# The order of the two readers of a score tile in the masked layers of a cross-attention stack

## Chip, cores and metric

The kernel runs on one core of a Trainium2 chip. The metric is device time in microseconds (us). Five engines work side by side, each through its own instructions in order: TensorE (PE in the profile; its weight loads are PEld), VectorE (DVE), ScalarE (ACT), GpSimd (POOL) and SyncE (SP, which issues DMAs). Semaphores hold an instruction back until those of other engines that it depends on are done.

## What is computed

Four cross-attention layers follow one another on an activation `x` of 2048 rows by 256, all of them attending to the same context of 1601 rows by 512. Layers 0, 2 and 3 are the masked ones; layer 1 is a grouped-query layer with an RMS norm. Cut to what matters here, a masked layer is:

```python
q = (x @ Wq).reshape(...)          # 16 heads of 64
k = (ctx @ Wk).reshape(...); v = (ctx @ Wv).reshape(...)
logits = einsum('bhqd,bhkd->bhqk', q, k) * 64 ** -0.5
col_bias[:, token_indices_A] = -20 * (1 - mask_A)[:, None]
col_bias[:, token_indices_B] = -20 * (1 - mask_B)[:, None]
probs = softmax(logits + col_bias, axis=-1)
x = (probs @ v).reshape(...) @ Wo + bo + x
```

All values are float32.

## The kernel before

**Tiling.** The activation stays in SBUF, transposed (`xT`). A masked layer is cut into 8 blocks, each a pair of heads `n`, and a block into 4 units, each 512 query rows; so there are 24 masked blocks and 96 masked units, and 32 units of the grouped layer. Scores are computed transposed: 128 keys on the partitions, and two heads by 512 queries in the free dimension. The keys of a layer, 1601 and 12 extra columns for the biased tokens, make `NT` = 13 key tiles (the last is shorter). `exc` holds a very negative number for the keys that a layer must leave out, so the score tile is never used without adding a column of `exc`.

**One key tile of a unit** passes through these steps:
- `front` (L393 to L411, matmuls L401; for the last key tile also the bias rows, L408): PE writes the score tile `s` in PSUM.
- `front_act` (L414): ACT copies the score tile to a slot `p` of an SBUF ring (L422). For key tile 0 it is instead an activation that adds `exc` (L418).
- `front_dve` (L424): DVE takes the running maximum, `top = max(s + exc, top)` (L430). For key tile 0 there is none; key tile 1 takes `p` of key tile 0 in place of `top`.
- `subtract`: 16 steps later DVE adds the negative maximum, spread over PSUM tile `mb`, to `p` in place (L461; L459 for key tile 0).
- `exp_act` and `exp_pool`: 18 steps later ACT takes the exponential in place (L467), and POOL adds it to `sums` (L473 for the first two tiles, L475 after).
- `attend`: 20 steps later PE multiplies it with the values into `po` (L483).

The score tile thus has two readers on two engines, L422 and L430. They are never run at the same time on one tile: whichever is written second in the program waits for the first, and the next `front` that uses the buffer waits for both.

**Other work of a unit.** PE transposes `top` (L439), DVE reduces it to `ntop` (L444), PE spreads it (L450) into `mb`. At the end of a unit ACT takes `po` out (`take`, L490); PE sums the exponentials over the keys (`row_pe`, L496); ACT evacuates them (`row_act`, L503), and they go through DRAM (`dens`) to a reciprocal on DVE (L512) and back into `rx`; POOL multiplies `o` by it (L523). PE then multiplies by `Wo` (`out_pe`, `halves`, L301) in two parts, and DVE adds each to `xT` (L566). The queries of a later unit are a matmul of `xq` (L301) that ACT scales into `qT` (L390). The keys and values of the next block are made meanwhile as "fill" pieces (L301), evacuated by ACT into `kT` (L351) and `v` (L371). In the last block of each layer the row piece is replaced by another form (`den_pe`, `den_act`, `scale_pe`).

**Buffers.** PSUM holds two score tiles (`ps_s`), one `mb`, one `po` and a single buffer `pm`, which all the smaller products share: a `pm` matmul waits until the one before it has been evacuated. The ring has 22 slots; a copy waits until POOL and PE have used what the slot held 22 tiles ago. There is one `sums`, so L473 of a unit waits for L496 of the unit before.

**Order.** Masked operations are pinned to program order (`pin`), and that order is written out by hand in the loop over `pair` (from L1060). A pair is two steps, so two key tiles; 13 pairs make two units. A small planner puts at most one piece in the middle of a pair (`mid`, `m` in the loop) and one at its end (`end`, `e`), by fixed offsets within the unit and, for fill, by how much is due. A piece has a PE part and may have a DVE part and an ACT part. The order within a pair, before the change, is: both fronts (PE); both `front_act` (ACT); sometimes one subtraction; the first `front_dve`; the middle piece's PE and DVE parts; the second `front_dve`; the middle piece's ACT part (`m.act`); the attends and `take`; the end piece's PE and DVE parts; the exponentials and sums; the end piece's ACT part; the subtractions. What stands on one engine runs in this order.

Of the kernel before, what the change touches and what calls it, by code (L numbers as in the profile page):

```python
# [38 lines left out]
def tile_cross_attention_stack(ctx: ExitStack, tc: tile.TileContext, t: dict, out: bass.AP):  # L39
# [874 lines left out]
    def at_step(s, offset):  # L914

        w, c = divmod(s - offset, NT)
        return (units[w], c) if 0 <= w < NU else None
# [127 lines left out]
    def plan_queries(w):  # L1045
        def pe():
            un = unit(w)
            un.qpe, un.qthen = un.layer.queries(un)
            un.qpe()

        if made[w // NB].layer.grouped:
            early.setdefault((NT * w - (2 if w % 32 == 0 else 12)) // 2, []).append(lambda: fetch(w))
            return
        early.setdefault(max(NT * w - 18, 0) // 2, []).append(lambda: fetch(w))
        place(end, NT * w - 6, Piece(1024, pe, act=lambda: units[w].qthen()))
# [4 lines left out]
    for pair in range((END + 1) // 2):  # L1060
        steps = [2 * pair, 2 * pair + 1]
        for s in steps:
            w, c = divmod(s, NT)
            if c == 0 and w < NU:
                i, b = divmod(w, NB)
                if b == 0:
                    made[i].layer.load_out(made[i])
                if b == 0 and i + 1 < len(blocks):
                    l, n = blocks[i + 1]
                    while i and fill:  # L1070
                        _, pe, then = fill.popleft()
                        pe()
                        then()
                    made[i + 1] = layers[l].load(n)
                    new = layers[l].fill(made[i + 1])
                    fill.extend(new)
                    total = sum(f[0] for f in fill)

                    hold = 9 if i and layers[blocks[i - 1][0]].grouped and n == 1 else 1
                    pace = total / (NB * NT / 2 - 3 - hold)  # L1080
                    due = -pace * hold
                    spent = 0.0
                plan(w)
                for v in ([1, 2] if w == 0 else [w + 2]):
                    if v < NU:
                        plan_queries(v)
        fronts = [at_step(s, 0) if s < NT * NU else None for s in steps]
        subs = [at_step(s, SUB) for s in steps]
        exps = [at_step(s, EXP) for s in steps]
        vals = [at_step(s, VAL) for s in steps]  # L1090
        fronts = [f for f in fronts if f]
        subs = [f for f in subs if f]
        exps = [f for f in exps if f]
        vals = [f for f in vals if f]

        due += pace
        if fill and spent + fill[0][0] <= due + 400:
            slot = mid if pair not in mid else end if pair not in end else None
            if slot is not None:
                cost, pe, then = fill.popleft()  # L1100
                spent += cost
                slot[pair] = Piece(cost, pe, act=then)
        m, e = mid.pop(pair, None), end.pop(pair, None)

        lead = len(vals) == 2 and vals[0][1] == NT - 1
        if lead:
            un, c = vals.pop(0)
            un.layer.attend(un, c)
            un.layer.take(un)
        for thunk in early.pop(pair, []):  # L1110
            thunk()
        grouped_back = [f for f in subs if f[0].layer.grouped]
        all_grouped = bool(fronts) and all(f[0].layer.grouped for f in fronts) and all(
            f[0].layer.grouped for f in subs) and bool(subs)
        for f in fronts + grouped_back:
            f[0].alone = all_grouped
        for i in range(2):
            for f in fronts[i : i + 1]:
                f[0].wide = False
                f[0].layer.front(*f)  # L1120
            if i == 0:
                for f in grouped_back[:1]:
                    f[0].wide = True
                    f[0].layer.again(*f)
        for f in fronts:
            f[0].layer.front_act(*f)
        for f in subs:
            if not f[0].layer.grouped and f[1] == NT - 1 and f is subs[0]:
                f[0].layer.subtract(*f)
                subs = subs[1:]  # L1130
                break
        for f in fronts[:1]:
            f[0].layer.front_dve(*f)
        if m:
            m.pe()
            if m.dve:
                m.dve()
        for f in fronts[1:]:
            f[0].layer.front_dve(*f)
        if m and m.act:  # L1140
            m.act()
        for un, c in vals:
            un.layer.attend(un, c)
            if c == NT - 1:
                un.layer.take(un)
        for f in grouped_back[1:]:
            f[0].wide = True
            f[0].layer.again(*f)
        if e:
            e.pe()  # L1150
            if e.dve:
                e.dve()
        for f in grouped_back:
            f[0].layer.exp_act(*f)
        for f in exps:
            if not f[0].layer.grouped:
                f[0].layer.exp_act(*f)
                f[0].layer.exp_pool(*f)
        if e and e.act:
            e.act()  # L1160
        for f in subs:
            if not f[0].layer.grouped:
                f[0].layer.subtract(*f)
# [34 lines left out]
```

## Time and profile before

| | |
|---|---|
| median of 3 runs | 4883.03 us (4873.75 to 4885.01) |
| the profiled execution | 4873.81 us |
| its span, first to last instruction | 4872.0 us |
| mean granted TensorE clock | 0.975 of full |
| copies L422 | 1152 of 1014 ns |
| running maxima L430 | 1056 of 1280 ns, and 96 of 1283 ns |
| subtractions L461 | 1152 of 1273 ns |
| exponentials L467 | 1248 of 1059 ns |
| sums on POOL L475 | 1056 of 2371 ns |
| ACT's evacuation of the sums `rx` L503 | 84, 0.6 us each |

The profile shows one execution. Its page gives each engine's busy time and the chain of work that ended last, followed back from the end; its groups put instructions of one line, engine and operation together. The trace behind it answers further views: who waited for whom, a timeline of stretches of time, and busy time by windows with the granted TensorE clock. A bracket in the timeline is the idle time of the engine before the instruction and what ended it.

The masked layers run from about 120 to 1320 us and from about 2320 us to the end; the grouped layer lies between, with both kinds of unit in flight at its edges.

### The profile page before, as it was taken

How to read it: one execution, taken by the hardware profiler on the slowest of the kernel's cores; microseconds unless marked ns; L12 is line 12 of the kernel's file. 1: busy time of each engine (PE TensorE's matmuls, PEld its weight loads, DVE VectorE, ACT ScalarE, POOL GpSimd, SP SyncE). 2: the span in 40 equal slices, each digit the busy share in tenths (PEclk: the TensorE clock that was granted, in tenths of full speed). 3: DMA queues.
4: the chain of work that ended last, by engine and by line, in shares of the span. 5: the costliest groups of instructions: out<-in, count | busy, mean ns of one | idle time of the engine just before them, and what ended most of it. 6: DMA issues, size and time to landing. Idle time of an engine off the chain costs nothing.

```text
span 4872.0 us, 68510 instructions
## 1 busy us (share of the span) xinstructions
PE 4510.9 (93%) x26779; PEld 1883.5 (39%) x26779; DVE 3779.4 (78%) x3687; ACT 3192.2 (66%) x3709; POOL 3012.8 (62%) x1565
## 2 busy tenths in 40 slices
PE   6999999999878989898999999999999999999997
PEld 3433443334333333334433443344433433344332
DVE  3788888888866666654788888888888888888896
ACT  2677676776645555555677666766666776767775
POOL 0677777777751222110677777777777777777787
PEclk8999999999989999999999999999999999999998
DMA  2000010100011000000000010001000001011000
GB/s 82 17 25 26 24 27 25 31 22 27 22 31 32 12 18 19 10 21 20 21 25 23 27 27 25 25 25 27 23 24 20 27 25 31 23 27 27 22 18 18
DMA packets 136793, 121.70 MB, mean 25 GB/s; under 512 B 64033, under 2 KB 103457, under 8 KB 136470
## 3 DMA queue, kind: packets, MB, share of 16 engines
q1 hardware_dynamic: 125238, 103.50, 7.8%
q0 software_dynamic: 9120, 11.72, 1.2%
q8 instruction: 212, 3.47, 0.3%
q10 hardware_dynamic: 2112, 2.10, 0.1%
q14 instruction: 111, 0.91, 0.1%
HBM read 103.16 MB, written 14.09 MB: 24 GB/s over the span
## 4 chain that ended last, share of the span: by engine, by line
PE 76%; ACT 10%; DVE 6%; POOL 4%; issue 3%; DMA 1%; POOLq 0%; SPq 0%; ACTq 0%; DVEq 0%
PE pm L301 21%; PE s L401 20%; PE po L483 17%; PE po L830 4%; ACT p L822 3%; ACT p L422 3%; DVE top L430 3%; POOL sums L473 2%; PE pm L439 2%; PE mb L450 2%; POOL sums L475 2%; PE s L760 1%; ACT p L467 1%; PE s L809 1%; DVE p L461 1%
## 5 line engine op out<-in xcount | busy, mean ns | idle before, releaser
L475 POOL TENSOR_TENSOR sums<-sums,p 128x1024 f32<-128x1024 f32 (+1 forms) x1056 | 2503.6, 2371 | 372.4 <-ACT p L467 319.7
L430 DVE SCALAR_TENSOR_TENSOR top<-s,exc,top 128x1024 f32<-128x1024 f32 (+1 forms) x1056 | 1351.7, 1280 | 408.3 <-ACT p L422 373.0
L422 ACT COPY p<-s 128x1024 f32<-128x1024 f32 (+1 forms) x1152 | 1129.4, 1014 | 664.5 <-PE s L401 461.8
L461 DVE SCALAR_TENSOR_TENSOR p<-p,exc,mb 128x1024 f32<-128x1024 f32 (+1 forms) x1152 | 1418.1, 1273 | 0.0
L401 PE MATMUL s<-qT,kT 64*128 64x512 f32 (+1 forms) x4992 | 1280.3, 622 | 94.8 <-DVE top L430 93.9
L467 ACT ACTIVATE p<-p 128x1024 f32<-128x1024 f32 (+1 forms) x1248 | 1255.2, 1059 | 23.2 <-DVE p L461 22.0
L483 PE MATMUL po<-p,v 128*64 128x512 f32 (+1 forms) x4992 | 1207.7, 600 | 3.5 <-ACT p L467 2.7
L401 PEld LDWEIGHTS s<-qT,kT 64*128 64x128 f32 (+1 forms) x4992 | 418.1, 184 | 774.5 <-issue 317.9
L473 POOL TENSOR_TENSOR sums<-p 128x1024 f32<-128x1024 f32 x96 | 226.8, 2363 | 732.2 <-PE pm L496 544.5
L483 PEld LDWEIGHTS po<-p,v 128*64 128x64 f32 (+1 forms) x4992 | 341.0, 138 | 540.8 <-issue 441.6
L775 DVE TENSOR_REDUCE gtop<-s 128x2 f32<-128x1024 f32 x261 | 316.8, 1221 | 123.7 <-PE s L760 122.5
L301 PE MATMUL pm<-wv,ctxT 128*64 128x128 f32 (+1 forms) x4992 | 361.5, 283 | 48.1 <-ACT rx L503 45.6
L742 POOL DMA_DIRECT2D qT<-gqueries x256 | 123.9, 492 | 454.9 <-PE s L814 296.3
L301 PEld LDWEIGHTS pm<-wv,ctxT 128*64 128x64 f32 (+1 forms) x4992 | 287.8, 139 | 203.4 <-issue 100.9
L822 ACT ACTIVATE p<-s 128x1024 f32<-128x1024 f32 (+1 forms) x267 | 270.1, 1023 | 138.8 <-PE s L814 134.8
L301 PE MATMUL pm<-ctxT,wk 128*64 128x256 f32 (+1 forms) x2688 | 314.2, 377 | 8.3 <-ACT rx L503 4.8
L301 PEld LDWEIGHTS pm<-ctxT,wk 128*64 128x64 f32 x2688 | 172.6, 140 | 199.3 <-issue 75.9
L830 PE MATMUL po<-p,v 128*32 128x512 f32 (+1 forms) x1664 | 245.3, 621 | 1.9 <-ACT rx L842 1.6
L301 PE MATMUL pm<-o,wo 128*64 128x512 f32 x768 | 205.2, 611 | 10.2 <-POOL o L523 6.1
L775 DVE TENSOR_REDUCE gtop<-mb 128x2 f32<-128x1024 f32 x123 | 150.3, 1222 | 75.1 <-PE mb L760 74.5
L444 DVE TENSOR_REDUCE ntop<-pm 128x4 f32<-128x512 f32 x192 | 131.8, 687 | 97.5 <-PE pm L439 97.1
L822 ACT ACTIVATE p<-mb 128x1024 f32<-128x1024 f32 (+1 forms) x149 | 152.5, 1024 | 77.9 <-PE mb L814 75.7
(165 smaller groups left out, 3226.4 us busy)
## 6 DMA issues: line engine op xcount, KB each, us to landing
xq<-snap SPq DMA_DIRECT2D x84, 512.0 KB
rx<-dens SPq DMA_DIRECT2D x168, 128.0 KB
qT<-gqueries POOLq DMA_DIRECT2D x256, 32.0 KB, 2.0
wk<-in_L_xattn_Wk_dram SPq DMA_DIRECT2D x24, 256.0 KB
wv<-in_L_xattn_Wv_dram SPq DMA_DIRECT2D x24, 256.0 KB
snap<-xT SPq DMA_DIRECT2D x12, 512.0 KB
gqueries<-xq SPq DMA_DIRECT2D x16, 256.0 KB
kT<-gkeys POOLq DMA_DIRECT2D x16, 200.2 KB, 3.9
```

What stands on the lines that cost most here:

```text
L301: pin(nc.tensor.matmul(to[a:e], weights_ap[:, a:e], moving, **kw))
L401: pin(nc.tensor.matmul(s[:m, h, :], u.kT[r, c * P : c * P + m], w.q[r, :], start=True, stop=(c < NT - 1),))
L422: pin(nc.scalar.copy(w.p[c][:m], w.s[c][:m]))
L430: pin(nc.vector.scalar_tensor_tensor(w.top[:m], w.s[c][:m], self.exc[:m, c : c + 1], before[:m], ALU.add, ALU.max,))
L461: pin(nc.vector.scalar_tensor_tensor(p, p, self.exc[:m, c : c + 1], w.mb[:m], ALU.add, ALU.add))
L467: pin(nc.scalar.activation(w.p[c][:m], w.p[c][:m], AF.Exp))
L473: pin(nc.gpsimd.tensor_tensor(w.sums, w.p[0], w.p[1], ALU.add))
L475: pin(nc.gpsimd.tensor_tensor(w.sums[:m], w.sums[:m], w.p[c][:m], ALU.add))
L483: pin(nc.tensor.matmul(w.po[r, :], w.u.v[:m, c, r], w.p[c][:m, h, :], start=(c == 0), stop=(c == NT - 1),))
L775: pin(nc.vector.tensor_reduce(w.top[:, :, q, k : k + 1], w.s[i], AX.X, ALU.max))
L822: pin(nc.scalar.activation(w.p[c][:m], w.s[c][:m], AF.Exp))
L830: pin(nc.tensor.matmul(w.po[ts(j, 32), :], self.v[:m, c, w.u.g, :], w.p[c][:m, h, :], start=(c < 2), stop=(c >= NT - 2),))
```

## The change

For each of the two score tiles of a pair, the running maximum (`front_dve`) now stands first and the copy (`front_act`) directly behind it, in place of both copies ahead of both maxima. Nothing else is written differently; for the grouped layer `front_act` does nothing.

```diff
@@ -1122,8 +1122,6 @@
                 for f in grouped_back[:1]:
                     f[0].wide = True
                     f[0].layer.again(*f)
-        for f in fronts:
-            f[0].layer.front_act(*f)
         for f in subs:
             if not f[0].layer.grouped and f[1] == NT - 1 and f is subs[0]:
                 f[0].layer.subtract(*f)
@@ -1131,12 +1129,14 @@
                 break
         for f in fronts[:1]:
             f[0].layer.front_dve(*f)
+            f[0].layer.front_act(*f)
         if m:
             m.pe()
             if m.dve:
                 m.dve()
         for f in fronts[1:]:
             f[0].layer.front_dve(*f)
+            f[0].layer.front_act(*f)
         if m and m.act:
             m.act()
         for un, c in vals:
```

The copy of a tile now depends on the maximum of that tile, where the maximum depended on the copy. A maximum of key tile 1 still needs the activation of key tile 0.

## The prediction

> **What bounds the kernel now.** I read the page first: busy times, then the chain that ended last.
>
> ```profile
> PE 4510.9 (93%) x26779; PEld 1883.5 (39%) x26779; DVE 3779.4 (78%) x3687; ACT 3192.2 (66%) x3709; POOL 3012.8 (62%) x1565
> PE 76%; ACT 10%; DVE 6%; POOL 4%; issue 3%; DMA 1%; POOLq 0%; SPq 0%; ACTq 0%; DVEq 0%
> ```
>
> TensorE (PE) is busy 93% and holds 76% of the chain. The masked layers alone, in the table by windows (us, then busy time of PE, PEld, DVE, ACT, POOL), are tighter still:
>
> ```profile
> 2500.00:2900.00 400.00, 383.63 (x2268) 160.90 (x2266) 331.33 (x300) 279.06 (x327) 295.81 (x131) 0.98 0.10 26
> ```
>
> PE 96%, DVE 83%, ACT 70%. So a change can give back at most the 4% that PE idles, but can cost as much as it makes PE wait. Who makes PE wait stands in the list of waits (total us, times, longest):
>
> ```profile
> DVE top L430 <- ACT p L422: 444.1, 330, 22.5
> ...
> PE s L401 <- DVE top L430: 93.9, 80, 7.6
> ...
> PE pm L301 <- ACT rx L503: 60.8, 63, 2.4
> ```
>
> The first is what the change removes: the maximum (L430) waits for the copy (L422) of its own score tile. It is idle time of DVE, not of PE. The second is PE waiting for a score buffer (there are two), which the maximum frees as last reader; the third is PE waiting for the single `pm` buffer.
>
> **The change.** In the instruction streams of both builds the counts agree, DVE's order and PE's order are the same, and the waits swap: each maximum waits for PE instead of ACT, each copy waits for DVE instead of PE. ACT's order is the same too, except that one square root of the grouped layer's norm comes a copy (1.0 us) earlier. On POOL three loads of that layer pass one sum, far from its bound (67 of 400 us busy in 1900 to 2300). On SP, 39 loads of `xq` go ahead of a read of `dens`; such a load waits until the queries have read the old `xq`, and the reciprocal that needs the read comes 7 us later on DVE (2817.03 to 2824.60), which covers it; uncovered, each would cost at most the 1 us by which the read is issued later, 39 in all. I count all three at nothing. So the whole price is who is late. Rows: maximum 1.28 us, copy 1.01, exponential 1.06, subtraction 1.27; back to back on one engine they start 1.19, 0.91, 0.96 and 1.19 apart, two dependent maxima 1.39. A handover from ACT to DVE takes 0.03 us (chain, below); from DVE to ACT none is shown; between 0.03 and the 0.24 that a weight load takes after DVE I take 0.04.
>
> *With both engines free* nothing changes: copy, maximum, maximum ends as late as maximum, maximum, copy (3.7 us). *With ACT late* the new order frees the buffer up to 1.3 us sooner. *With DVE late* the copy, until now done in DVE's shadow, is put behind the maximum: the buffer comes free 1.0 us later, and everything queued behind the copies on ACT (evacuating `pm`, the exponentials) comes later by up to 2 to 4 us. DVE is the fuller engine, so I followed one turn of the schedule, 13 pairs of steps (two units, about 80 us), pair by pair, with the durations above. Nine pairs hide it: for example at 2817.36 copies end at 2822.8 instead of 2820.5, the next front needs that buffer at 2823.8, and the exponentials end at 2825.1, before their products at 2826.8. Four do not.
>
> ```profile
> 2804.16 1.99 PE L401 MATMUL s<-qT,kT 64*128 64x512 f32 x8
> ...
> 2807.09 2.66 DVE L430 SCALAR_TENSOR_TENSOR top<-s,exc,top 128x1024 f32<-128x1024 f32 x2
> ...
> 2808.07 0.37 ACT L351 COPY kT<-pm 128x256 f32<-128x256 f32 x1 [0.75 <-PE pm L301]
> ...
> 2809.57 1.03 PE L301 MATMUL pm<-o,wo 128*64 128x512 f32 x4
> ...
> 2814.07 2.67 DVE L430 SCALAR_TENSOR_TENSOR top<-s,exc,top 128x1024 f32<-128x1024 f32 x2 [0.35 <-ACT p L422]
> ...
> 2814.83 0.61 ACT L503 COPY rx<-pm 128x512 f32<-128x512 f32 x1
> ...
> 2815.49 1.94 PE L301 MATMUL pm<-xq,wq 128*64 128x512 f32 x8 [0.25 <-ACT rx L503]
> ```
>
> (1) The front at 2804.16. DVE's maxima of the pair before, with the `xT` addition between them, end at 2802.8 and 2804.6; the second copy then ends at 2805.7, where PE wanted that buffer at 2805.1: **+0.6**. (2) The exponentials follow until 2807.6; this pair's maxima end at 2808.2 and 2809.5 (DVE first does two subtractions), the copies at 2809.2 and 2810.6, the `kT` copy behind them at 2810.9 instead of 2808.4. PE's output matmul needs that `pm` at 2809.6 + 0.6: **+0.7**. (3) That matmul now ends at 2811.9, so the addition, two subtractions and two maxima on DVE run to 2817.6; the second copy to 2818.7, the `rx` copy to 2819.2 instead of 2815.4. PE's queries wait for `pm`: 2819.2 against 2815.5 + 1.3 already lost: **+2.4**, a standstill of 2.7 us. Sum 3.7.
>
> ```profile
> 2837.84 1.27 DVE L430 SCALAR_TENSOR_TENSOR top<-s,exc,top 128x1024 f32<-128x1024 f32 x1
> ...
> 2839.64 1.27 DVE L430 SCALAR_TENSOR_TENSOR top<-s,exc,top 128x1024 f32<-128x1024 f32 x1
> ...
> 2841.06 1.13 PE L401 MATMUL s<-qT,kT 64*128 64x512 f32 x4 [0.71 <-DVE top L430]
> ```
>
> (4) Here DVE is behind (three subtractions, an addition), and PE already waits 0.71 us. The copies were done at 2836.7; now they start at 2839.2 and 2840.95, so the two fronts begin at 2840.2 and 2842.0: **+0.94**. The exponentials end at 2843.9, the next copies at 2845.7, `kT` at 2845.9; where the piece is the short one (77 columns) the output matmul waits **0.5** more. In the next pair DVE's subtractions wait for that matmul; maxima end at 2852.65, the second copy at 2853.7, the `v` copy at 2854.0, and the queries, ready at 2852.4, wait **1.65**. Sum 2.6 or 3.1, mean 2.9.
>
> A turn loses 3.7 + 2.9 = 6.6 us. There are 96 masked units, 48 turns; I take 46, since the last block of a layer has another row piece and the last of all no fill: **46 x 6.6 = 304 us**.
>
> What it gains: the chain once per two turns,
>
> ```profile
> 2938.93 2.35 POOL sums L473
> ...
> 2941.31 1.02 ACT p L422
> ...
> 2942.36 1.29 DVE top L430
> ...
> 2943.70 1.13 PE s L401 x4
> ```
>
> a copy waits for POOL to free a ring slot, the maximum for the copy, PE for the maximum. The maximum would now be done, and PE resumes at 2942.4: 1.3 us sooner, a standstill of 0.85 instead of 2.17. What is late next is POOL's product `o` (L523), which the output matmul needs 16 us on: in blocks where PE ran at full clock after this stall that matmul already waits 0.6 us for it (599.92), so nothing is kept there; where the clock fell, about 1.0 us is. 11 x 1.0 = **-11 us**. The other such chain, which ends in the `rx` copy (the 2.40 us stalls), has no maximum in it and stays.
>
> The clock after a stall, by windows (the figure before the last two is the granted clock):
>
> ```profile
> 2941.50:2944.90 3.40, 1.23 (x8) 0.45 (x8) 2.54 (x3) 3.40 (x5) 3.20 (x2) 1.00 0.00 1
> 2944.90:2948.30 3.40, 3.40 (x18) 1.95 (x18) 3.30 (x3) 1.63 (x2) 3.32 (x2) 0.50 0.04 1
> ```
>
> Of 44 stalls of 2.17 to 2.41 us in the masked layers, 23 are followed by 3.4 us at half clock, 1.7 us each; of the shorter ones (up to 0.79), none. So the 46 new stalls of 2.7 us, a little longer, bring about 46 x 0.55 x 1.7 = **+43 us** (bounds: none, 78 if each does), and the 11 shortened ones that had it (of 22) give back 11 x 1.7 = **-19 us**.
>
> The Trainium skill ("TensorE: Matmul & The Clock Gate", HAM oscillation) warns of idle gaps over about 3.4 us; the rows above fall to half after 2.17. By the page's figure alone both clock terms would be nothing and the sum 5167. The skill also speaks for the wait itself ("PSUM — Partial Sum Buffer", PSUM bank collisions raise a hardware error): ScalarE and VectorE may not read one bank at once; so one reader must wait either way, as both builds do.
>
> **Sum.** The profiled execution took 4873.8 us (span 4872.0), the lowest of the three timed runs being 4873.75 and the median 4883.03. 4873.8 + 304 - 11 + 43 - 19 = 5191; I say **5190**.
>
> **Rivals.**
> A, *faster*: ACT is the late reader, not DVE. Its place is the PE waits behind the maximum, 93.9 us, and the half clock after them, 19: at most -113, so 4761; if only the ring chain gains, 22 x 1.3 + 19 = 48, 4826. It decides if at step (3) the maxima can start over 1 us before the old 2814.07. For it: 444 us of DVE waiting. Against: DVE's additions and subtractions stand between, and most of those waits are 0.35 to 0.6 us in front of an engine with 17% to spare. Chance 0.07.
> B, *no change* (4860 to 4888): the shifts end in PE's slack, as in nine pairs of 13. It needs (1) to (4) each to be over 0.6 to 2.4 us too long. 0.06.
> C, *front waits only*: (1) and (4)'s 0.94 stay, but `pm` comes free in time at (2), (3) and (4): 46 x 1.54 = 71, so 4945; with half of the other 233 some 5060. 0.14.
> D, *more*: each copy's 1.05 us lands on PE in each pair, 624 x 1.05 = 655, so 5530, or delayed exponentials also hold up POOL's sums and `o`: some 5330. 0.07.
> The forecast, 5080 to 5290: 0.66.
>
> **Range.** 5030 to 5290: the forecast with its clock bounds and the upper half of C, short of D. Faster by over 0.3% (about what can be told from no change here) 0.08, within 0.06, slower 0.86.
>
> **What would show it.** Right: DVE's wait for the copy gone from the list, in its place ACT's copy waiting for the maximum with over 400 us; PE waiting for `rx` (L503), `kT`/`v` copies and the score copy with 250 to 350 us in all; standstills of about 2.7 us before the queries, twice a block, with half clock after many; the 2.17 us stalls at 0.9. Wrong: if the queries start without a wait, (3) failed; if fronts wait no longer than 0.71, (4) failed; if the exponentials reach the products late, a fifth place was missed.

## The result and the profile after

The changed kernel takes 5239.74 us (median of 4 runs, 5233.25 to 5241.64) against 4880.42 before: a ratio of 1.0735, with a 95% interval of 1.0716 to 1.0754. It is slower by some 360 us. The profiled execution has a span of 5238.6 us, 366.6 more than that of before.

The page after, busy times and the chain that ended last:

```profile
PE 4592.7 (88%) x26779; PEld 1870.8 (36%) x26779; DVE 3781.8 (72%) x3687; ACT 3198.3 (61%) x3709; POOL 3011.2 (57%) x1565
...
PE 41%; DVE 16%; ACT 9%; issue 4%; POOL 3%; DMA 0%; ACTq 0%; POOLq 0%; DVEq 0%; SPq 0%
```

DVE, ACT and POOL are busy for the same time as before to 6 us: no instruction got dearer. PE is busy 82 us longer with the same 26779 matmuls, and its share of the chain falls from 76% to 41%: the chain now leaves PE often, above all for DVE (16% from 6%).

The list of waits after (total us, times, longest):

```profile
ACT p L422 <- DVE top L430: 1210.9, 920, 6.1
...
DVE top L430 <- PE s L401: 428.1, 226, 8.7
...
PE pm L301 <- ACT rx L503: 164.0, 63, 2.8
...
PE s L401 <- ACT p L422: 116.4, 149, 4.7
```

and, further down the same list, three more waits of PE:

```profile
PE pm L301 <- ACT kT L351: 60.9, 65, 1.7
...
PE pm L301 <- POOL o L523: 42.3, 25, 3.1
...
PE pm L301 <- ACT v L371: 41.4, 45, 1.7
```

The maximum's wait for the copy (444 us) is gone, as the change says. DVE gained nothing: it now waits 428 us for PE. The wait came back on ACT, nearly three times as long, and what stands behind ACT's copies came back as waits of PE: `rx` 164 us from 61, and `kT` and `v` 102 from 5. PE waits for the score buffer 116 us instead of 94.

The place where the forecast put most of the loss, in the timeline after (start, us, engine, line; the last PE row is the queries):

```profile
2984.65 2.67 DVE L430 SCALAR_TENSOR_TENSOR top<-s,exc,top 128x1024 f32<-128x1024 f32 x2
...
2988.31 0.38 ACT L351 COPY kT<-pm 128x256 f32<-128x256 f32 x1
...
2988.74 1.08 PE L301 MATMUL pm<-o,wo 128*64 128x512 f32 x4 [1.02 <-ACT kT L351]
...
2992.85 2.67 DVE L430 SCALAR_TENSOR_TENSOR top<-s,exc,top 128x1024 f32<-128x1024 f32 x2
...
2995.61 1.01 ACT L422 COPY p<-s 128x1024 f32<-128x1024 f32 x1 [0.38 <-DVE top L430]
2996.52 0.59 ACT L503 COPY rx<-pm 128x512 f32<-128x512 f32 x1
...
2997.16 3.27 PE L301 MATMUL pm<-xq,wq 128*64 128x512 f32 x8 [2.70 <-ACT rx L503]
```

The second copy starts when the second maximum ends (2995.5); `rx` starts when ACT is done with the copy; the queries start when `rx` is out. PE stood still 2.70 us, where it was 0.25, and the queries then took 3.27 us instead of 1.94: the clock had fallen. All matmuls of the queries together, from the groups before and then after (busy time and mean duration, then PE's idle time before them and what ended it):

```profile
L301 PE MATMUL pm<-xq,wq 128*64 128x512 f32 x672 | 160.6, 599 | 12.5 <-ACT rx L503 10.4 <-DVE parts L650 2.0
```

```profile
L301 PE MATMUL pm<-xq,wq 128*64 128x512 f32 x672 | 201.4, 729 | 176.7 <-ACT rx L503 113.3
```

Since both kernels run the same matmuls in the same order, the two traces can be laid side by side matmul by matmul, and each growth of the lag put to the place where it arises:

| lag that arises at | us | forecast |
|---|---|---|
| the queries, waiting for `rx`, `kT`, `v` | +170.7 | 46 x (2.4 + 1.65) = 186 |
| the fronts, waiting for the score copy | +61.4 | 46 x (0.6 + 0.94) = 71 |
| the output matmul, waiting for `kT`, `v` | +44.2 | 46 x (0.7 + 0.25) = 44 |
| matmuls without a wait (half clock, above all) | +39.9 | +43 - 19 = 24 |
| the 2.17 us stalls, shortened | -31.8 | with the next row: -11 |
| the output matmul, waiting for POOL's `o` | +37.0 | |
| the edge of grouped and masked layers | +20.2 | none |
| the rest of the grouped layer, and others | +25 | none |

### The profile page after: what moved, and what is told of

Its sections match the earlier page's. It is cut to its first block, busy times and chain, and to the rows that moved or that the text cites. A ratio compares the mean times of both kernels' runs of the same rounds, so it can differ in the third digit from the quotient of the medians.

```text
span 5238.6 us, 68422 instructions
## 1 busy us (share of the span) xinstructions
PE 4592.7 (88%) x26779; PEld 1870.8 (36%) x26779; DVE 3781.8 (72%) x3687; ACT 3198.3 (61%) x3709; POOL 3011.2 (57%) x1565
## 4 chain that ended last, share of the span: by engine, by line
PE 41%; DVE 16%; ACT 9%; issue 4%; POOL 3%; DMA 0%; ACTq 0%; POOLq 0%; DVEq 0%; SPq 0%
PE pm L301 11%; PE s L401 9%; PE po L483 7%; DVE top L430 7%; DVE p L461 6%; PE po L830 4%; ACT p L422 3%; ACT p L822 3%; POOL sums L473 1%; PE s L760 1%; ACT p L467 1%; PE pm L439 1%; POOL sums L475 1%; PE s L809 1%; PE mb L809 1%
## 5 line engine op out<-in xcount | busy, mean ns | idle before, releaser
L422 ACT COPY p<-s 128x1024 f32<-128x1024 f32 (+1 forms) x1152 | 1159.5, 1013 | 1341.9 <-DVE top L430 1210.9
L401 PE MATMUL s<-qT,kT 64*128 64x512 f32 (+1 forms) x4992 | 1298.4, 628 | 118.2 <-ACT p L422 116.4
L822 ACT ACTIVATE p<-s 128x1024 f32<-128x1024 f32 (+1 forms) x267 | 270.1, 1023 | 142.1 <-PE s L814 138.1
L301 PE MATMUL pm<-xq,wq 128*64 128x512 f32 x672 | 201.4, 729 | 176.7 <-ACT rx L503 113.3
L301 PE MATMUL pm<-ctxT,wk 128*64 128x256 f32 (+1 forms) x2688 | 303.6, 368 | 8.4 <-ACT rx L503 4.8
L566 DVE TENSOR_TENSOR xT<-pm,xT 128x512 f32<-128x512 f32 x168 | 115.3, 686 | 216.3 <-PE pm L301 216.2
```

Source lines behind the costliest of these rows:

```text
L301: pin(nc.tensor.matmul(to[a:e], weights_ap[:, a:e], moving, **kw))
L401: pin(nc.tensor.matmul(s[:m, h, :], u.kT[r, c * P : c * P + m], w.q[r, :], start=True, stop=(c < NT - 1),))
L422: pin(nc.scalar.copy(w.p[c][:m], w.s[c][:m]))
L822: pin(nc.scalar.activation(w.p[c][:m], w.s[c][:m], AF.Exp))
```

## The experiments

**e1: the piece's ACT part ahead of the copies.** The maxima stay first; ACT evacuates `pm` before it copies the scores.

```diff
         for f in fronts[:1]:
             f[0].layer.front_dve(*f)
-            f[0].layer.front_act(*f)
+            if f[1] == 0:
+                f[0].layer.front_act(*f)
         if m:
             m.pe()
             if m.dve:
                 m.dve()
+            if m.act:
+                m.act()
+        for f in fronts[:1]:
+            if f[1]:
+                f[0].layer.front_act(*f)
         for f in fronts[1:]:
             f[0].layer.front_dve(*f)
             f[0].layer.front_act(*f)
-        if m and m.act:
-            m.act()
```

> The changed kernel, but ACT runs the middle piece's part (the copies that free pm: rx, kT, v) ahead of the two score copies instead of behind them; maxima still go first. Theory (DVE is the late reader, and most of the loss is pm held up by evacuations queued behind the late copies): the waits for rx, kT and v fall to almost nothing, the 2.7 us standstills and their half clock go, the 2.40 us stall behind the ring goes too; the score-buffer waits of about 1.0 and 0.6 us a turn stay, and qT, now later behind the exponentials, costs up to 0.9. Some 4900 to 5000 us. Rival (the score buffer itself, held 1 us longer by the copy, is the loss): unchanged within 30 us of 5240, since the copies come later still.

Measured 4994.27 us, ratio to before 1.024 (1.0219 to 1.0261), within what the theory gave and 245 us below the changed kernel. Its list of waits:

```profile
ACT p L422 <- DVE top L430: 553.7, 449, 5.2
...
PE s L401 <- ACT p L422: 83.8, 117, 4.7
PE pm L301 <- POOL o L523: 82.6, 82, 3.0
...
PE pm L301 <- ACT qT L390: 42.2, 45, 1.0
...
PE po L483 <- ACT p L467: 36.4, 48, 1.9
```

No wait of PE for `rx` or `kT` stands among them. The rival, the score buffer alone, is out: the copies come later still, and two thirds of the loss are gone. The 245 us are not a clean share of `pm`, though. Laid beside the kernel before, matmul by matmul, e1 has also lost 75 us of waits for `rx` that the kernel before has itself (e4 below takes them out alone), and its own order brings new waits. What the change itself had added at `pm` is the 215 us of the table above (170.7 and 44.2). What is left of the loss (117 us by the traces) lies elsewhere than expected: the exponentials, later still, hold up POOL's sums and with them `o` (82.6 us), and the products with the values (36.4); and evacuating the queries into `qT`, now behind the exponentials, holds up `pm` (lag of 58 us).

**e2 and e3: half of the change.** In e2 the maximum goes first for the first tile of a pair only, in e3 for the second only.

```diff
 # e2
         for f in fronts[1:]:
-            f[0].layer.front_dve(*f)
             f[0].layer.front_act(*f)
+            f[0].layer.front_dve(*f)
...
 # e3
         for f in fronts[:1]:
-            f[0].layer.front_dve(*f)
             f[0].layer.front_act(*f)
+            f[0].layer.front_dve(*f)
```

> One part of the change alone: the maximum goes first for the first tile of each pair, for the second tile the copy stays first. Theory (two engines that hand over to each other in both directions): the second copy stands behind the first copy, which stands behind the first maximum, and the second maximum waits for the second copy, so DVE, which is late already, loses about 1.5 us a pair in addition: by my working 4.3 us in the first half of a turn where the whole change lost 3.7, so 5200 to 5350 in all. Rival (each swapped tile costs its own share): about half the loss, some 5060.

> The other part alone: the copy first for the first tile of each pair, the maximum first for the second. Theory: the exponentials stand behind the late second copy, the next pair's first copy behind the exponentials, and the next first maximum waits for that copy, so DVE is made later from pair to pair: worse than the whole change, 5300 to 5550. Rival (each swapped tile costs its own share): about half the loss, some 5060.

Measured 5439.65 us (1.1165, 1.1132 to 1.1198) and 5680.66 us (1.1646, 1.1622 to 1.167). Each half of the change costs more than the whole; both lie above my ranges, by 90 and 130 us. The waits of e2 show why:

```profile
ACT p L422 <- DVE top L430: 1454.2, 537, 9.6
DVE top L430 <- ACT p L422: 1079.2, 528, 22.9
```

Now each engine waits for the other in most pairs (537 and 528 waits in 624 pairs), and I read this as delays that no longer run side by side but after one another. That the price is not a share per swapped tile is shown. The sizes I had underrated; I had followed one turn from an undisturbed start and not the lag that one turn hands to the next, but that this is the reason is not shown.

**h: the same change with DVE relieved.** In both orders the subtraction works on one of the tile's two heads only, and the exponential scales its input so that it stays finite, so part of the softmax is left out.

```diff
-            p = w.p[c][:m]
+            p, mb = w.p[c][:m, 0], w.mb[:m, 0]
             if c == 0:
-                pin(nc.vector.tensor_tensor(p, p, w.mb[:m], ALU.add))
+                pin(nc.vector.tensor_tensor(p, p, mb, ALU.add))
...
-            pin(nc.scalar.activation(w.p[c][:m], w.p[c][:m], AF.Exp))
+            pin(nc.scalar.activation(w.p[c][:m], w.p[c][:m], AF.Exp, scale=1e-3))
```

> The kernel before with DVE relieved: the subtraction works on one of the two heads of a tile only (half the columns), and the exponential scales its input by 0.001 so that it stays finite; the output is not the reference's. It is the base for the next run. DVE loses some 0.55 us in each of 13 subtractions of a unit. Theory: PE is the bound, so only the 0.71 us stalls and part of the 2.17 go: 4800 to 4870. Rival (DVE bounds the kernel): 4600 or less.

> The changed kernel with the same relief of DVE (half the subtraction left out, exponential scaled). Theory (the loss comes from DVE being the late reader): with DVE early the order of the readers nearly stops to matter; by my working 1.4 us before the queries and 0.7 in the other unit remain, so 60 to 110 us above the run with the copy first, against 360 without the relief. Rival (a copy behind a maximum costs its 1 us wherever DVE stands): 300 to 360 us above.

Measured 4825.64 us with the copy first and 5000.77 with the maximum first: 175 us apart, against 360 without the relief. The direction is the theory's, the size neither's. Laid side by side, the three forecast waits (queries, fronts, output behind `kT` and `v`) cost 86 + 4 + 12 = 102 us here, where I had worked out 97; with the unrelieved DVE they cost 276. In the maximum-first run the output matmul and the queries wait like this:

```profile
L301 PE MATMUL pm<-o,wo 128*64 128x512 f32 x768 | 208.3, 621 | 54.2 <-POOL o L523 42.8 <-ACT kT L351 6.6 <-DVE xq L726 1.9
...
L301 PE MATMUL pm<-xq,wq 128*64 128x512 f32 x672 | 162.6, 604 | 92.1 <-ACT rx L503 69.0 <-ACT kT L351 10.7 <-ACT v L371 10.2
```

(the last figures are PE's idle time before the group and what ended it). The queries wait 92 us, most of it for `rx`. What I left out stands in the first line: the 30 us that the ring stalls give back are taken again by POOL's `o`, and the layer edge costs 18 here too. Some 45 us more arise at matmuls that wait for nothing, which I did not trace to a cause. So with DVE relieved half of the loss is gone, and of the three forecast waits 174 of 276 us: that much of it is DVE's lateness, shown. The queue of maximum, maximum, copy, evacuation holds PE's queries up even with this relief.

**e4 and e5: a better order.** If what stands behind a copy on ACT is the matter, the kernel before has such a place too: the 2.40 us stalls, where the copy waits for the ring and `rx` stands behind it. e4 moves that one evacuation ahead of the second copy in pairs with the row piece; e5 also lets the maximum go first for the second tile where the first is key tile 8, the one pair where the copy waits for the ring. Against the kernel before, with a mark `row` on the row piece:

```diff
+        row = m is not None and m.row
-        for f in fronts:
+        for f in fronts[: 1 if row else 2]:
             f[0].layer.front_act(*f)
...
             m.pe()
             if m.dve:
                 m.dve()
+            if row:
+                m.act()
+        late = row and fronts and fronts[0][1] == 8
         for f in fronts[1:]:
+            if row and not late:
+                f[0].layer.front_act(*f)
             f[0].layer.front_dve(*f)
-        if m and m.act:
+            if late:
+                f[0].layer.front_act(*f)
+        if m and m.act and not row:
             m.act()
```

(In e4 the second copy follows `m.act()` in every such pair.)

> The kernel before with one move: in pairs with the row piece, ACT evacuates pm into rx ahead of the second score copy instead of behind it. Theory (what is queued behind a copy on ACT sets PE): the 2.40 us stalls, where the copy waits for the ring and rx stands behind it, go, and the 0.25 us waits before the queries: 22 x 2.4 + 42 x 0.25, and some half clock, less a new wait of 0.6 for the score buffer: 50 to 85 us faster, 4795 to 4830. Rival (POOL's chain from sums to o is the next limit): no more than 20 us faster.

> As the run before, and the maximum first for the second tile of those row pairs alone whose first tile is key tile 8, where the copy waits for the ring and DVE does not. Theory (the maximum pays to go first where ACT is the late reader): the 2.17 us stalls shrink to 0.85, half of it taken back by POOL's o: 10 to 30 us faster than the run before. Rival (maximum first always costs): slower than the run before.

Measured 4803.73 us (0.9839, 0.9826 to 0.9853) and 4786.71 us (0.9807, 0.9794 to 0.982): both in their ranges, e5 17 us below e4, and 96 us faster than the kernel before on the same chip (4882.38). The waits of DVE and PE around the maximum in e5's list, and the group of the output matmul from its page (busy time and mean duration, then PE's idle time before it and what ended it):

```profile
DVE top L430 <- ACT p L422: 326.3, 235, 24.6
...
PE s L401 <- DVE top L430: 61.2, 77, 7.6
```

```profile
L301 PE MATMUL pm<-o,wo 128*64 128x512 f32 x768 | 205.2, 610 | 28.6 <-POOL o L523 24.8
```

No matmul waits for `rx` any more. Laid beside e4, e5's 2.17 us stalls give back 26 us, and `o` (21) and a later `v` (11) take all of it again; that e5 is faster all the same lies in the matmuls that wait for nothing, which gain 20 us. This is the clock: 13 of e4's 22 such stalls are followed by half clock, and the masked layers have 72 us at half clock in e4's records and 38 in e5's, so 17 us less lost. So the maximum does pay to go first, in the one pair where ACT is the late reader, and little there, because POOL is next; by these two profiles, what it keeps is the clock.

**e6 and e7: the layer edge.** e6 is the changed kernel, but with both copies first in pairs that also run the second half of a grouped unit; e7 is the changed kernel again, on the same chip.

```diff
+        edge = bool(grouped_back)
+        for f in fronts if edge else []:
+            f[0].layer.front_act(*f)
         for f in fronts[:1]:
             f[0].layer.front_dve(*f)
-            f[0].layer.front_act(*f)
+            if not edge:
+                f[0].layer.front_act(*f)
...
```

> The changed kernel, but in pairs that also run the second half of a grouped unit (the edge from layer 1 to layer 2) both copies go ahead of both maxima again. Theory (a fifth place that the prediction missed: there the grouped exponential stands behind the copies on ACT, and PE waits for the single mb buffer that it frees): 15 to 24 us faster than the changed kernel on the same chip, all of it near the end of the grouped layer. Rival (those 24 us are half clock and phase, not this wait): within 6 us of it.

> The changed kernel once more, as the base of the run before: 5240 us, within 8.

Measured 5233.72 us (1.0729, 1.0712 to 1.0746) and 5239.15 (1.0748, 1.0733 to 1.0763): 5.4 us apart, with intervals that overlap. By the times this is undecided; my 15 to 24 us are not confirmed, and the rival's "within 6 us" is what they show. In the traces the place itself is settled. The group of matmuls that wait for the `mb` buffer there, in the kernel before, in e6 and in e7:

```profile
L809 PE MATMUL mb<-qT,kT 64*128 64x512 f32 (+1 forms) x298 | 71.3, 474 | 13.4 <-ACT p L822 9.2 <-DVE gtop L775 4.2
```

```profile
L809 PE MATMUL mb<-qT,kT 64*128 64x512 f32 (+1 forms) x298 | 71.6, 476 | 13.4 <-ACT p L822 9.2 <-DVE gtop L775 4.2
```

```profile
L809 PE MATMUL mb<-qT,kT 64*128 64x512 f32 (+1 forms) x298 | 73.0, 486 | 24.5 <-ACT p L822 20.3 <-DVE gtop L775 4.2
```

The idle time before it, 13.4 us, is that of the kernel before again, and the lag that arises in this stretch falls from 23 us to 4. Of these 19 us, 10 are lost again behind it, in matmuls that wait for nothing (45 us of lag in e6's profile, 35 in e7's). The records of the granted clock explain these 10: from the last grouped matmul to the end e6 has 144 us at half clock and e7 120, and half of the difference is 12. In the lag, then, the edge is worth what I expected, and in these two profiles the clock takes half of it back.

## Why the prediction was right, and where its sizes were off

**The direction and the cause** were right: DVE is the late reader, the copy lost DVE's shadow, and PE pays. The laying side by side and e1 show the part of `pm`, h that of DVE's lateness (about half), e5 that the opposite holds where ACT is late. The waits named as a sign of being right came to more than said: `rx`, `kT`, `v` and the score copy hold PE up for 383 us in the list, not 250 to 350.

**Steps (1) to (4)** held at the place where they were worked out. In the next block of the same kind the lag grows by 0.7 us at the front of (1) (forecast 0.6), by 0.6 and 1.2 at the output matmul of (2) (0.7), by 2.45 at the queries of (3) (2.4), by 1.05 at the fronts of (4) (0.94), by 0.5 at the short piece's output matmul (0.5) and by 1.7 to 1.8 at the queries after it (1.65). Step (4) in the timeline after:

```profile
3023.59 1.13 PE L401 MATMUL s<-qT,kT 64*128 64x512 f32 x4 [0.98 <-ACT p L422]
...
3025.40 1.13 PE L401 MATMUL s<-qT,kT 64*128 64x512 f32 x4 [0.68 <-ACT p L422]
...
3029.24 1.08 PE L301 MATMUL pm<-o,wo 128*64 128x512 f32 x4 [0.31 <-ACT kT L351]
...
3037.45 1.94 PE L301 MATMUL pm<-xq,wq 128*64 128x512 f32 x8 [1.52 <-ACT v L371]
```

Over the kernel they sum to 276 us, not 304: in the blocks where the output matmul first waits for `o`, PE is late already and step (1) finds its buffer free, and the queries with a row piece come 42 times, not 46.

**The gain** was mis-sized. The 2.17 us stall did shrink, as worked out, to 0.88. In the chain after, the maximum has dropped out, and PE resumes 0.04 us after the copy:

```profile
3132.48 2.38 POOL sums L473
...
3134.88 1.02 ACT p L422
...
3135.94 1.13 PE s L401 x4
```

But 17 us later the output matmul stands and waits for POOL's product `o` (PE's timeline after):

```profile
3149.52 1.99 PE L401 MATMUL s<-qT,kT 64*128 64x512 f32 x8
3153.41 1.08 PE L301 MATMUL pm<-o,wo 128*64 128x512 f32 x4 [1.90 <-POOL o L523]
```

The shortened stalls gave back 31.8 us, and the half clock that 11 of them had brought, 11 x 1.7 = 19; `o` took 37.0 again. That leaves -14, where the forecast had -30. The term that was wrong is the second of "-11 us" and "-19 us": where POOL sets when PE goes on, what PE saves before that point, clock included, counts once, and the -11 was already what `o` lets PE keep. Without the -19 the forecast would have been 5210.

**The clock** came out near its term, in part by luck. The queries stand still for 2.70 us in the forecast place 41 times, and 29 of these are followed by half clock (0.71, where I took 0.55): 29 x 1.7 = 49 us against 43. But the 22 stalls of 2.41 us behind `rx`, which the change does not shorten, and whose clock the forecast left as it was, did not keep theirs: 12 of them were followed by half clock before, and only 1 after, some 11 x 1.7 = 19 us in the change's favour. So a share of stalls, carried over from one kernel to another, is not a safe term. The windows after, one stall and the two stretches behind it (the granted clock is the figure before the last two):

```profile
2993.80:2997.20 3.40, 0.70 (x6) 0.04 (x2) 3.29 (x4) 2.60 (x4) 1.50 (x1) 1.00 0.00 0
2997.20:3000.60 3.40, 3.40 (x10) 0.89 (x12) 0.70 (x1) 1.94 (x3) 2.35 (x1) 0.56 0.00 1
3000.60:3004.00 3.40, 3.40 (x22) 1.62 (x24) 2.04 (x2) 1.24 (x2) 2.35 (x1) 0.94 0.52 160
```

PE is busy throughout the second, at 0.56 of its clock; the queries in it took 3.27 us instead of 1.94. On this point the trace decides against the figure of the Trainium skill ("TensorE: Matmul & The Clock Gate", HAM oscillation), idle gaps over about 3.4 us: by that figure alone no such stall would have cost anything more.

**A fifth place was missed**: the edge between a grouped layer and a masked one, +20.2 us. There the grouped layer's exponential (L822) is queued on ACT behind the late copies, and PE waits for the one `mb` buffer, 10 us longer than before; e6 shows it. I had followed one turn in the middle of a masked layer only. So the way from the forecast's 317 us to the 366.6 measured is: the steps 28 less; clock and gain together +45 instead of +13; the edge 20; and some 25 in the rest of the grouped layer and in small places, which I did not trace to a cause. Part of it is the clock: between the first and the last grouped matmul the records have 99 us at half clock after and 68 before, which is 15 us lost, in this rest and in the edge together.

**The rivals.** A, *faster*: 444 us of DVE waiting was idle time of an engine that had other work to come late with; it is gone and nothing was gained by it. The point from which A decides, ACT being the late reader, exists in one pair (e5). B, *no change*, and C, *front waits only*, fell with steps (2) and (3): the fronts are 61 of 366.6 us. D, *more*, was half right in its second part: the delayed sums and `o` did hold PE up, by 37 us, but not by the price of a copy in each pair.

## What to carry to other kernels

Where two engines must read one buffer in turn, let the one go first that is less late, and price the order not by the wait between the two but by what is queued behind the second reader on its own engine, above all evacuations of a buffer of which there is only one. Such an evacuation pays to be moved ahead of anything that may wait for a slow engine: moving one took 1.6% off this kernel, and the swap of readers in the one pair where the copy is the late one another 0.3%. Keep one order for all tiles between the same two engines, unless a trace shows which one is late where: each half of this change cost more than the whole.

## What the runs showed of the hardware that was not expected

Half clock follows short stalls, not always, and not by their length alone. Stalls of 2.17 us in the kernel before have it in 11 of 22 cases, those of 2.70 us in the changed kernel in 29 of 41, and those of 1.52 to 1.68 us before its queries in none of 38. But the stall of 2.41 us behind `rx`, which both kernels have, is followed by it in 12 of 22 cases before, in 1 of 22 after and in none of 22 in e7; the same stall, of 2.4 to 2.5 us, in the maximum-first run of h in 19 of 20. What decides it besides the length, no run here shows. Each time it lasted about 3.4 us and cost 1.7.

A sum of half clock over a whole profile is not a sum of lost time. Executions of one kernel differ in it: 297 us in the first profile of the changed kernel (span 5238.6 us), 380 in e7's (5247.1). Of the difference, 55 us lie in the first 70 us of the program, where they cost nothing that can be seen: from 20 to 70 us the granted clock is 1.00 in the first and 0.50 in the second, and PE is busy for 25.2 and 25.4 of the 50 us. Taken by stages, as for e6 above, the sums fit the lags better.
